# One core, attention and FFN: the last five blocks of the down weights looked up one at a time, and a higher look-up rate in gate and up

## The chip, the core and the metric

The kernel runs on one NeuronCore of a Trainium2 chip. It is one program with five instruction streams: PE (matrix multiplies into PSUM), DVE (element-wise work and all table look-ups), ACT (activations, copies out of PSUM and casts), POOL (here little more than the DMAs that it issues) and SP (most DMAs). The streams run side by side and wait for each other by semaphores; each works through its own instructions in the order in which they were written. The metric is the device time of one execution in microseconds. The time before is the median of three runs, 1115.92 us (1115.61 to 1116.86).

## The reference

The input x is 2 x 2048 x 512 in float32. A layer norm, an attention over the feature axis (the scores are 512 x 512 for each batch) and a residual come first. The feed-forward part follows, and its weights are not given as numbers but as indices into a table of 16 values:

```python
def _ghost_linear(x, idx, lut):
    w = lut[idx]
    return jnp.einsum('bsh,oh->bso', x, w)
...
gate = _ghost_linear(x, gate_idx, lut)      # gate_idx: 1376 x 512, values 0..15
up = _ghost_linear(x, up_idx, lut)          # up_idx: 1376 x 512
h = jax.nn.silu(gate) * up
return _ghost_linear(h, down_idx, lut)      # down_idx: 512 x 1376
```

The result is x + attention(norm(x)), and to that the feed-forward part of its norm is added.

## The kernel before

**Stages.** The program runs through the norm and the Gram matrices of x, a few products of 512 x 512 matrices, the attention's output y for 32 blocks of rows, then gate and up, then down. Products are made by Winograd's form of Strassen's scheme: a product of two-by-two blocks takes seven multiplies instead of eight, and sums of the operands (S1 to S4 for the left one, T1 to T4 for the right one) that DVE makes beforehand.

**Gate and up.** The 1376 inner features are cut into 11 blocks (`FT`, line 84; ten of 128 and one of 96); f counts them from 0. For each f there are four units, one for each pair p of chunks of rows (`GateUp`, line 819). A unit has seven stages: a1, c1, a2, c2, b, a3 and a4, each one product of two matrix multiplies 512 columns wide. `Line.run` (line 884) writes them in the order a1, c1, a4 of the unit before, a2, c2, b, a3. After each stage it calls `between`. Beside the products, ACT copies results out of PSUM (p1, p7, u2) and makes the two SiLUs (h0, h1); DVE makes the add for c21 and the product for h1 at stage c2, the add for h0 at stage b, and the add for c22 and the product for h0 at stage a3. The product a4 is written into the PSUM bank that c22's add reads. SP stores h to DRAM, and down reads it back.

**The look-ups.** A job (`Job`, line 191) turns up to 1024 columns of indices into weights. POOL fetches the indices by DMA (`fetch`, two buffers), ACT casts them to 16 bits (`cast`), and DVE then runs 19 instructions (`ops`): two masks in 16 bits (one step), a shift, a third mask, eight picks (a `tensor_scalar` that chooses between two neighbours of the table by the lowest bit of the index) and seven merges (a `copy_predicated` on a mask). A gate-and-up job `gu(f)` looks up a block's gate and up weights, 1024 columns (768 for the last block), and makes four sums of them. A down job `wd` looks up two blocks of 512 columns each (one for the last).

**The order of the work.** It is written out by hand. The list `jobs` (lines 300 to 302) fixes the order of the look-ups. `looked_up` (line 304) is a generator which hands out one DVE step at a time with an estimated cost in microseconds. `pump(us)` (line 321) adds us to a credit and takes steps until the credit is used up; the last step may overshoot, and the overshoot is owed:

```python
owed[0] = min(owed[0] + us, 2 * us + 1.0)
while owed[0] > 0:
    cost = next(lookup, None)
    if cost is None:
        return
    owed[0] -= cost
```

A job `gu(f)` has a gate: it may start only once block f-2 has been written out (`f < 2 + passed[0]`, line 282), since there are two buffers for a block's weights. While the gate is closed the list stands, and `pump` returns. Tenth step of a job (`k == 9`): the next job's indices are cast. End of a job: the indices of the job two further on are fetched.

`between` (line 917) runs a prepared piece of other work if there is one (20 of them, all in block 0), and else calls `pump`. At the start of block f the loop (line 1095) makes sure that the weights are there, by handing out whatever is left of the list up to them, without any stage of PE between:

```python
while "S4" not in gu[f]:
    next(lookup)
```

The down weights are first used in the sums at the start of the last block of gate and up (`down_sums`, line 951).

Of the kernel before, what the change touches and what calls it, by code (L numbers as in the profile page):

```python
# [58 lines left out]
def tile_attn_ffn(  # L59
# [24 lines left out]
    FT = [(f, min(P, INTER - f)) for f in range(0, INTER, P)]  # L84
    NFT = len(FT)
    NPAIR = NFT // 2
# [20 lines left out]
    wd = wdp.tile([P, NFT, E], F32, tag="wd", name="wd")  # L107
# [143 lines left out]
    def gu_job(f):  # L251
        f0, rows = FT[f]
        n = KB * rows

        def load(queue, idx):
            queue.dma_start(idx[:, :n], gate_idx[:, KB * f0 : KB * f0 + n])
            queue.dma_start(idx[:, n:], up_idx[:, KB * f0 : KB * f0 + n])

        def dest():
            gu[f] = {  # L260
                "w": wgu.tile([P, 2, KB, P], F32, tag="w", name=f"w_{f}"),
                "s": wgu.tile([P, 3, 2, P], F32, tag="s", name=f"s_{f}"),
            }
            flat = gu[f]["w"].rearrange("p g k r -> p (g k r)")[:, : 2 * n]
            gu[f]["flat"] = flat
            return flat

        def after():
            flat = gu[f]["flat"].rearrange("p (g k r) -> p g k r", g=2, k=KB)
            a11, a12 = flat[:, 0, 0:2, :], flat[:, 0, 2:4, :]  # L270
            a21, a22 = flat[:, 1, 0:2, :], flat[:, 1, 2:4, :]
            s1, s2, s4 = (gu[f]["s"][:, q, :, :rows] for q in range(3))
            for op, d, u, v in (
                (add, s1, a21, a22), (sub, s2, s1, a11), (sub, a21, a11, a21), (sub, s4, a12, s2)
            ):
                op(d, u, v)
                yield 0.42
            gu[f].update(
                {"11": a11, "12": a12, "S3": a21, "22": a22, "S1": s1, "S2": s2, "S4": s4}
            )  # L280

        return Job(f"gu{f}", P, 2 * n, load, dest, after, lambda: f < 2 + passed[0])

    def down_job(i):
        f0, rows = FT[2 * i]
        n = 2 if i < NPAIR else 1

        def load(queue, idx):
            queue.dma_start(
                idx.rearrange("p (o e) -> p o e", o=n),  # L290
                down_idx[f0 : f0 + n * rows, :].rearrange("(o p) e -> p o e", o=n),
            )

        def dest():
            return wd[:rows, 2 * i : 2 * i + n, :].rearrange("p o e -> p (o e)")

        return Job(f"wd{i}", rows, n * E, load, dest, lambda: iter(()), lambda: True)


    jobs = [gu_job(0), gu_job(1)] + [down_job(i) for i in range(3)]  # L300
    jobs += [gu_job(2), gu_job(3), down_job(3), gu_job(4), down_job(4), gu_job(5), gu_job(6)]
    jobs += [down_job(NPAIR)] + [gu_job(f) for f in range(7, NFT)]

    def looked_up():

# [15 lines left out]
    def pump(us):  # L321
# [7 lines that stand above are left out]
# [555 lines left out]
    class Line:  # L884


        def __init__(self, between):
            self.last, self.between = None, between
# [28 lines left out]
    def between():  # L917
        if todo:
            todo.pop(0)()
        else:  # L920
            pump(0.9)


    def late(i, loads=(), turns=(), pair=None):
# [163 lines left out]
    def by_two(ops):  # L1088
        return [
            lambda v=ops[i : i + 2]: [op() for op in v] for i in range(0, len(ops), 2)  # L1090
        ]

    line = Line(between)
    for f in range(NFT):
        while "S4" not in gu[f]:
# [102 lines left out]
```

## Time and profile before

| what | value |
|---|---|
| median of three runs | 1115.92 us (1115.61 to 1116.86) |
| the profiled execution, its own time | 1115.62 us |
| its span, first to last instruction | 1113.8 us |
| mean granted PE clock | 0.995 |
| busy: PE, DVE, ACT, POOL | 1089.8, 695.1, 303.6, 32.1 us (98%, 62%, 27%, 3%) |
| HBM traffic over the span | 105 GB/s |

The profile's page splits the span among the engines, and lists the costliest groups of instructions by the line that made them. In the groups' names, a_g, b_g and c_g are the PSUM tiles of gate and up, a_d, b_d and c_d those of down, w and s a block's weights and their sums, gu and wd the tiles of the look-ups, and idx, b the indices in 32 and 16 bits. Line 814 is the helper that issues the multiplies, lines 125 and 128 the helpers for a difference and a sum, line 230 the pick and line 242 the merge. Each multiply in float32 shows as two records, so a stage of gate and up is four. In a line of waits, the three figures are the total in us, how many times, and the longest. The time outside the span, 1115.62 - 1113.8 = 1.8 us, is the start and end of the execution.

### The profile page before, as it was taken

To read this page: it belongs to the slowest core of one execution; us is meant where nothing else is said; L and a number is where in the kernel's file an instruction comes from. 1 tells how busy PE (TensorE), PEld (TensorE's weight loads), DVE (VectorE), ACT (ScalarE), POOL (GpSimd) and SP (SyncE) were. 2 spreads that over 40 slices of the span, in tenths; PEclk is the share of its full clock that TensorE was granted. 3 is DMA by queue.
4 is the path that set the end of the run, shared out by engine and by line. 5 is a ranking of instruction groups with operands and counts; after the bars stand their busy time and mean duration, and the time that the engine had idled before them with its cause. 6 is when DMAs were issued, how large, how long until landed. Compare 5 with 4: busy or idle time off the path is not lost.

```text
span 1113.8 us, 10427 instructions
## 1 busy us (share of the span) xinstructions
PE 1089.8 (98%) x3516; PEld 654.0 (59%) x3516; DVE 695.1 (62%) x1267; ACT 303.6 (27%) x567; POOL 32.1 (3%) x63
## 2 busy tenths in 40 slices
PE   7999999999999999999699999999999999999998
PEld 4668886444444444444244444444437888888887
DVE  6967787777576587788687675755552344433341
ACT  4642522565532223223122222222221000000000
POOL 0000000000230000000000000000000000000000
PEclk9999999999999999999899999999999999999999
DMA  8461203445741111111021111111315543345511
GB/s 339 174 223 46 50 19 109 157 131 184 257 154 38 67 66 39 61 61 66 26 67 67 56 48 62 39 47 48 137 49 178 161 156 129 103 161 169 159 64 38
DMA packets 80116, 117.15 MB, mean 105 GB/s; under 512 B 16432, under 2 KB 36912, under 8 KB 78144
## 3 DMA queue, kind: packets, MB, share of 16 engines
q1 hardware_dynamic: 76848, 106.99, 28.3%
q0 software_dynamic: 3216, 9.51, 2.9%
q8 instruction: 27, 0.44, 0.2%
q14 instruction: 25, 0.20, 0.1%
HBM read 64.56 MB, written 51.90 MB: 105 GB/s over the span
## 4 chain that ended last, share of the span: by engine, by line
PE 92%; DVE 3%; DMA 3%; ACT 1%; issue 1%; SPq 0%; POOL 0%; DVEq 0%; POOLq 0%; ACTq 0%
PE a_g L814 25%; PE a_d L814 14%; PE c_g L814 13%; PE y L686 9%; PE c_d L814 7%; PE gp L372 6%; PE b_g L814 6%; PE b_d L814 4%; DMA fl<-xnd 2%; PE ea_t L521 1%; PE ea_p L521 1%; PE ea_m L521 1%; PE ea_s L521 1%; PE xt L718 1%; PE ec_t L521 1%; PE ec_m L521 1%
## 5 line engine op out<-in xcount | busy, mean ns | idle before, releaser
L128 DVE TENSOR_TENSOR c<-c_g,u 128x512 f32<-128x512 f32 (+1 forms) x44 | 30.3, 690 | 142.9 <-PE c_g L814 136.1
L686 PE MATMUL y<-m,nT 128*128 128x512 f32 x256 | 112.8, 592 | 0.0
L814 PE MATMUL a_g<-xb,w 128*128 128x512 f32 (+1 forms) x176 | 84.6, 604 | 9.6 <-DVE w L242 9.6
L814 PE MATMUL c_g<-xb,w 128*128 128x512 f32 (+1 forms) x176 | 84.1, 600 | 1.4 <-DVE w L125 0.8
L814 PE MATMUL a_g<-xb,s 128*128 128x512 f32 (+1 forms) x176 | 82.9, 593 | 1.0 <-DVE c L128 1.0
L814 PE MATMUL a_g<-xT_a,s 128*128 128x512 f32 (+1 forms) x176 | 82.8, 592 | 0.0
L814 PE MATMUL b_g<-xb,w 128*128 128x512 f32 (+1 forms) x176 | 82.7, 592 | 0.0
L372 PE MATMUL gp<-xn_a 128*128 128x512 f32 (+3 forms) x256 | 71.7, 443 | 7.1 <-ACT xn_a L183 7.1
L686 PEld LDWEIGHTS y<-m,nT 128*128 128x128 f32 x256 | 47.4, 190 | 52.7 <-issue 52.1
L866 ACT ACTIVATE h<-h 128x512 f32<-128x512 f32 (+1 forms) x44 | 27.7, 630 | 166.3 <-DVE h L128 166.3
L372 PEld LDWEIGHTS gp<-xn_a 128*128 128x128 f32 x256 | 44.9, 195 | 33.5 <-issue 16.5
L814 PEld LDWEIGHTS a_g<-xb,w 128*128 128x128 f32 (+1 forms) x176 | 33.4, 191 | 53.0 <-issue 42.3
L814 PE MATMUL a_g<-xT_sq,s 128*128 128x512 f32 (+1 forms) x132 | 62.0, 592 | 0.0
L814 PEld LDWEIGHTS c_g<-xb,w 128*128 128x128 f32 (+1 forms) x176 | 33.4, 191 | 45.8 <-issue 42.2
L230 DVE TENSOR_SCALAR gu<-idx_gu,lut_x,lut_sb 128x1024 int32<-128x1024 int32 (+1 forms) x77 | 59.2, 795 | 0.0
L814 PEld LDWEIGHTS a_g<-xb,s 128*128 128x128 f32 (+1 forms) x176 | 32.8, 188 | 44.4 <-issue 38.6
L814 PEld LDWEIGHTS b_g<-xb,w 128*128 128x128 f32 (+1 forms) x176 | 33.0, 188 | 42.5 <-issue 42.5
L814 PEld LDWEIGHTS a_g<-xT_a,s 128*128 128x128 f32 (+1 forms) x176 | 32.9, 188 | 42.7 <-issue 42.0
L242 DVE COPY_PREDICATED gu<-b_gu,gu 128x1024 f32<-128x1024 int16 (+1 forms) x44 | 56.3, 1280 | 0.8
L814 PE MATMUL a_d<-dT,hs_a 128*128 128x256 f32 x224 | 56.2, 379 | 0.0
L242 DVE COPY_PREDICATED wd<-b_wd,wd 128x1024 f32<-128x1024 int16 (+1 forms) x42 | 51.0, 1215 | 0.7
L843 ACT COPY p<-a_g 128x512 f32<-128x512 f32 (+1 forms) x44 | 25.7, 584 | 83.7 <-PE a_g L814 83.7
(240 smaller groups left out, 1726.2 us busy)
## 6 DMA issues: line engine op xcount, KB each, us to landing
hd<-h SPq DMA_DIRECT2D x80, 256.0 KB, 2.0
h<-hd SPq DMA_DIRECT2D x40, 512.0 KB, 6.5
nl<-nd SPq DMA_DIRECT2D x128, 64.0 KB, 2.1
x1d<-x SPq DMA_DIRECT2D x8, 1024.0 KB, 4.5
r<-x1d SPq DMA_DIRECT2D x32, 256.0 KB, 4.2
out_dram<-r SPq DMA_DIRECT2D x32, 256.0 KB, 2.5
x<-in_x_dram SPq DMA_DIRECT2D x7, 1024.0 KB, 13.4
nd<-xn_a SPq DMA_DIRECT2D x20, 256.0 KB, 2.1
```

The costliest lines, as they stand in the source:

```text
L128: nc.vector.tensor_tensor(dest, a, b, ALU.add)
L230: vec.tensor_scalar(dest.bitcast(I32), idx, lut_x[:rows, k : k + 1], lut_i[:rows, at : at + 1], ALU.bitwise_and, ALU.bitwise_xor,)
L242: vec.copy_predicated(dest, masks[level - 1], t)
L372: nc.tensor.matmul(gp[b][i][:, i * P :], xn[:, i * P : (i + 1) * P], xn[:, i * P :], start=c % CPB == 0 and j == 0, stop=c % CPB == CPB - ...
L521: nc.tensor.matmul(ps[:, m, :], self.a[a][:, k, m * P : (m + 1) * P], self.b[b][:, k, :], start=first and m == k == 0, stop=k == 1, skip_g ...
L686: nc.tensor.matmul(ys[k], nTs[k][:, i, :], m[:, i, :], start=(i == 0), stop=(i == KB - 1))
L718: nc.tensor.transpose(ps[:, i * P : (i + 1) * P], xfs[k][:, i * P : (i + 1) * P], ident)
L814: nc.tensor.matmul(ps, lhsT, rhs, start=first and i == 0, stop=i == len(pairs) - 1, skip_group_check=not first,)
L843: nc.scalar.copy(self.p1, self.a)
L866: nc.scalar.activation(self.h0, self.h0, AF.Silu)
```

## The change

Two things change. First, the down weights of blocks 0 to 5 are still looked up in three jobs of two blocks each, but blocks 6 to 10 are now looked up in five jobs of one block (before: blocks 6 and 7, 8 and 9 in two jobs of two, block 10 in one). `down_job` takes the first block and the number of blocks. The new order of the list after the first five jobs is gu2, gu3, wd6, gu4, wd7, gu5, wd8, gu6, wd9, gu7, wd10, gu8, gu9, gu10; before it was gu2, gu3, wd6-7, gu4, wd8-9, gu5, gu6, wd10, gu7, gu8, gu9, gu10. Second, `between` pays 1.0 instead of 0.9 for each stage.

```diff
-    def down_job(i):
-        f0, rows = FT[2 * i]
-        n = 2 if i < NPAIR else 1
+    def down_job(i, n=1):
+
+        f0, rows = FT[i]
...
-            return wd[:rows, 2 * i : 2 * i + n, :].rearrange("p o e -> p (o e)")
+            return wd[:rows, i : i + n, :].rearrange("p o e -> p (o e)")
...
-    jobs = [gu_job(0), gu_job(1)] + [down_job(i) for i in range(3)]
-    jobs += [gu_job(2), gu_job(3), down_job(3), gu_job(4), down_job(4), gu_job(5), gu_job(6)]
-    jobs += [down_job(NPAIR)] + [gu_job(f) for f in range(7, NFT)]
+    jobs = [gu_job(0), gu_job(1)] + [down_job(i, 2) for i in range(0, 6, 2)] + [gu_job(2)]
+    for i in range(6, NFT):
+        jobs += [gu_job(i - 3), down_job(i)]
+    jobs += [gu_job(f) for f in range(NFT - 3, NFT)]
...
         if todo:
             todo.pop(0)()
         else:
-            pump(0.9)
+            pump(1.0)
```

## The prediction

> **What bounds the kernel now.** I read the page's busy shares first: PE 98%, DVE 62%, ACT 27%, a mean PE clock of 0.995. So PE sets the end, and only PE's gaps can be won. Second, the waits of PE between 340 and 840 us, the stretch of gate and up:
>
> ```profile
> PE a_g L814 <- DVE w L242: 9.6, 1, 9.6
> PE c_g L814 <- DVE w L125: 0.8, 1, 0.8
> PE a_g L814 <- DVE c L128: 0.8, 1, 0.8
> ```
>
> Two of the three are waits for w, the looked-up weights of a gate-and-up block; the third, 0.8, is the last product at 837 us, which the change does not touch. Third, the chain of waits around them (start, us, what):
>
> ```profile
> 477.60 3.43 PE a_g L814 x8
> ...
> 488.30 0.35 DVE w L125
> 488.65 0.04 issue
> 488.69 1.98 PE c_g L814 x4
> 490.68 3.43 PE a_g L814 x8
> ...
> 526.73 3.43 PE a_g L814 x8
> ...
> 538.12 1.29 DVE gu L242
> ...
> 543.53 1.31 DVE w L242
> 544.84 0.04 issue
> 544.88 3.78 PE a_g L814 x4
> 548.66 2.84 PE c_g L814 x4
> 551.50 3.43 PE a_g L814 x8
> ```
>
> A stage (one product) is four records and 1.72 us; a unit is seven stages, and its marker, an eight-record a_g (a4 and a2), returns every 12.02 us (502.69, 514.71, 526.73). A block is four units, 48.07 us. Block 4 begins near 486 us, block 5 near 535: 477.60 to 490.68 is 13.08, so 1.06 is lost; 526.73 to 551.50 is 24.77, so **12.75** is lost. Together **13.8 us**. From 551.50 to the marker at 827.89 are 276.39 us, exactly 23 units; nothing else is lost. Fourth, busy times by stretch (width; PE, PEld, DVE, ACT, POOL busy; PE clock; DMA share; GB/s):
>
> ```profile
> 392.00:440.00 48.00, 48.00 (x113) 21.28 (x112) 38.26 (x54) 13.75 (x23) 1.11 (x2) 1.00 0.15 55
> 536.00:545.00 9.00, 0.12 (x1) 0.12 (x1) 8.83 (x11) 0.67 (x1) 0.53 (x1) 0.75 0.15 51
> 545.00:548.70 3.70, 3.70 (x5) 1.63 (x6) 3.67 (x10) 0.00 (x0) 0.00 (x0) 0.50 0.02 4
> ```
>
> While PE stands, DVE does nothing but look-ups, and PE then restarts at half clock: the 12.75 is 9.57 of standing plus (3.78-1.72)+(2.84-1.72) = 3.18 of slow products. In block 2 (392 to 440), with DVE at 38.26 of 48, PE lost nothing.
>
> **Why DVE is late there.** The kernel's own costs say it. A gate-and-up job is 0.74+0.65+0.37, eight picks of 0.75, seven merges of 1.27, four sums of 0.42: 18.33 us. A two-block down job is the same without sums, 16.65; a one-block job has the same 19 instructions at half width: 0.47+0.375+0.235+8x0.475+7x0.685 = 9.68. A block pays 28 stages x 0.9 = 25.2. gu(f) may begin only in block f-1, and what stands behind it in the list waits too. Block 1: gu2, then gu3 is not yet allowed, 6.9 unused. Block 2: gu3 and 6.87 of wd3. Block 3: 9.78 of wd3 and 15.42 of gu4, 2.9 missing less the last step's overshoot: two sums are forced out at block 4 (the 1.06). Block 4: wd4, 16.65, then half of gu5; 9.0 forced out at block 5 (the chain shows just these merges). Later blocks carry at most 20.4.
>
> [...] 0.50 in 545 to 548.7 after 9.57 us; the 0.8 us gap cost no clock. [...] pick 808 ns at 1024 columns, 537 at 512; merge 1312 and 731. [...] In this trace, amid look-ups, the index DMAs issue in 0.53 to 0.85 us and land in 3.1 to 4.0 (medians)[...].
>
> **The change part by part.**
>
> ```profile
> L242 DVE COPY_PREDICATED wd<-b_wd,wd 128x1024 f32<-128x1024 int16 x14 | 18.4, 1312 | 0.3
> L230 DVE TENSOR_SCALAR wd<-idx_wd,lut_x,lut_sb 128x1024 int32<-128x1024 int32 x16 | 12.4, 808 | 0.0
> ...
> L242 DVE COPY_PREDICATED wd<-b_wd,wd 96x512 f32<-96x512 int16 x7 | 5.1, 731 | 0.2
> ...
> L230 DVE TENSOR_SCALAR wd<-idx_wd,lut_x,lut_sb 96x512 int32<-96x512 int32 x8 | 4.0, 537 | 0.0
> ```
>
> *Splitting.* Blocks 6 to 9 go from two wide jobs to four narrow ones; block 10 was narrow. By durations a wide job is 2x0.421+0.69+0.42+8x0.808+7x1.312 = 17.6, a narrow one 2x0.284+0.42+0.28+8x0.537+7x0.731 = 10.7 (measured on 96 rows; I take the same for 128, bounds 10.7 and, no cheaper than its columns, 8.8). DVE gains 38 instructions and 4x10.7-2x17.6 = +7.6 us. ACT gains two casts net: four at 0.62 for two at 1.05, +0.4. POOL gains two index DMAs at 0.7: +1.4. The first five jobs and gu2 keep their places, so nothing before 344 us moves.
>
> *Order and rate.* A block now has 28.0 to spend and, in blocks 2 to 6, gu(f+1) with one narrow job: 28.01; blocks 1 and 7 to 9 hold gate and up alone. At the start of a block the credit is up to 3.0, because the gate had stopped the list. Going through list and stages, gu(f+1) ends at stage 15 of 28 and the narrow job at 25; nothing is forced out at any boundary, with 12 stages, 20 us, in hand. Both gaps go: **-13.8**. After block 9 no job is left, as before, so the rate does nothing in down.
>
> *What hides the additions.* DVE in block 1, with gu2 alone, is 30.34 us busy; a narrow job adds 10.7 by durations, and 9.8 after the overlap that block 1's total shows (33.0 by durations for 30.34). So 40.2 of 48.07: 84%, 1.9 above block 2, where PE lost nothing. Cost on the path 0; were there no cover, 7.6.
>
> *The order on DVE.* More look-ups now stand in front of the adds that free PSUM. The tightest: a4 overwrites the bank that the add of c22 reads, two stages (3.43) after a3. From the end of c2, DVE does two operations (1.2), one stage's look-ups, h0 (0.6), another stage's, then c22 (0.7). Two stages' look-ups are at most 2.0 plus an overshoot of 1.3. So c22 ends at 5.8 at the latest, and a4 begins at 3.43+3.43 = 6.87: 1.1 in hand. DVE must be free at the end of c2: its idle time there is now 1.5 to 3.0 in looked-up stretches, less 7x0.1 = 0.7. Cost 0, bound 0.2 a unit.
>
> *Fetches.* ACT's cast of the next job stands in front of ACT's copies of PSUM. The index DMA goes out after the last pick of the job two before; from there to the cast are, after a gate-and-up job, 3.81+1.68+5.03 = 10.5 us of cost, 18 us of stages, against 2x0.54+3.5 = 4.6. After a narrow job it is 2.06+8.57, as long. Cost 0.
>
> Sum: the profiled execution, 1115.62, less 13.8 is 1101.8 (span 1100.0); the median of the runs shown lies 0.3 above the profiled one: **1102.0**. What is late next is nothing on DVE: PE runs back to back from 344 us to the end.
>
> **Rivals.** *A new wait on PSUM in place of the old ones.* DVE at 84% makes c22 late by some 0.2 us in each of 20 units of blocks 2 to 6: +4, 1106. For: DVE is in order, and the margin 1.1; against: block 2 at 38.26 without a gap. *A cast waits for its indices:* ACT stands until the fetch lands. PE stops once ACT is 3.4 late; five casts, each 0.5 beyond that, give 2.5: 1104.5. Against: 18 us of lead. *Slower: DVE becomes the bound of blocks 2 to 6.* It decides once their look-ups and adds need over 48.07 us; to eat the gain and 2.2 more takes 3.2 a block, a DVE need of 51.3, so a narrow job of some 21 us, twice the measured row. It would give 1118. *The forced look-ups stay* (the list is held elsewhere than I count): 1116.
>
> **How the numbers follow.** Forecast 0.84, PSUM wait 0.06, cast 0.05, DVE bound 0.02, gaps stay 0.03. The forecast alone spans 1101 to 1103.5; the low end takes 1 us for the runs' spread (1115.61 to 1116.86), the high end the cast and most of the PSUM case: 1100.7 to 1105.0. 0.2%, 2.2 us, is about what can be told from no change. Faster 0.95, same 0.03, slower 0.02.
>
> **What would show it.** PE's waits for w gone from the stretch; markers 12.02 us apart from 344 us on; no clock under 1.00 near 540; DVE about 40 busy in blocks 2 to 6; span near 1100. Wrong if PE waits for c L128 in many units, if ACT waits at its cast for a DMA, or if a wait for w remains at a block's start.

## The result and the profile after

The changed kernel takes **1101.64 us** (median of four runs, 1100.71 to 1102.65), the kernel before 1115.76 in the same comparison: a ratio of 0.9879, 95% interval 0.9867 to 0.9891. The profiled execution took 1100.71 us with a span of 1098.9. The forecast was 1102.0, in a range of 1100.7 to 1105.0.

The waits of PE in the stretch of gate and up, all of them (total in us, times, longest):

```profile
PE a_g L815 <- DVE c L128: 0.8, 1, 0.8
PE c_g L815 <- DVE xb L125: 0.4, 1, 0.4
```

The two waits for w are gone. What is left is the last product of gate and up, which was there before, and 0.4 us in block 0. (The helper of the multiplies is now line 815, since the diff adds a line.)

The chain of waits over the place of both old gaps (start, us, what):

```profile
488.67 3.43 PE a_g L815 x8
...
500.69 3.43 PE a_g L815 x8
...
512.70 3.43 PE a_g L815 x8
...
524.72 3.43 PE a_g L815 x8
...
536.74 3.43 PE a_g L815 x8
```

The marker of a unit comes every 12.02 us, through the starts of blocks 4 and 5 too. No line of DVE is in this part of the chain.

The busy times by stretch (width; PE, PEld, DVE, ACT, POOL; PE clock; DMA share; GB/s):

```profile
344.00:392.00 48.00, 48.00 (x114) 21.21 (x113) 30.33 (x44) 12.87 (x21) 0.56 (x1) 1.00 0.14 50
392.00:440.00 48.00, 48.00 (x113) 21.23 (x112) 39.37 (x63) 13.38 (x22) 1.62 (x3) 1.00 0.17 60
...
536.00:584.00 48.00, 48.00 (x113) 21.28 (x112) 39.42 (x63) 13.39 (x22) 1.60 (x3) 1.00 0.16 59
```

PE is busy throughout at full clock. DVE works 39.4 of 48 us in every block with a down job, and 30.3 in a block without.

### The profile page after: what moved, and what is told of

The parts are those of the page before. It is cut to its first block, busy times and chain, and to the rows that moved or that the text cites. A ratio compares the mean times of both kernels' runs of the same rounds, so it can differ in the third digit from the quotient of the medians.

```text
span 1098.9 us, 10474 instructions
## 1 busy us (share of the span) xinstructions
PE 1085.8 (99%) x3516; PEld 652.9 (59%) x3516; DVE 699.5 (64%) x1305; ACT 303.9 (28%) x569; POOL 32.9 (3%) x65
## 4 chain that ended last, share of the span: by engine, by line
PE 93%; DMA 3%; DVE 2%; ACT 1%; issue 1%; SPq 0%; POOL 0%; DVEq 0%; POOLq 0%; ACTq 0%
PE a_g L815 26%; PE a_d L815 14%; PE c_g L815 13%; PE y L687 9%; PE c_d L815 7%; PE gp L373 6%; PE b_g L815 6%; PE b_d L815 4%; DMA fl<-xnd 2%; PE ea_t L522 1%; PE ea_p L522 1%; PE ea_m L522 1%; PE ea_s L522 1%; PE xt L719 1%; PE ec_t L522 1%; PE ec_p L522 1%
## 5 line engine op out<-in xcount | busy, mean ns | idle before, releaser
L128 DVE TENSOR_TENSOR c<-c_g,u 128x512 f32<-128x512 f32 (+1 forms) x44 | 30.3, 690 | 120.7 <-PE c_g L815 120.7
L242 DVE COPY_PREDICATED wd<-b_wd,wd 128x512 f32<-128x512 int16 (+2 forms) x56 | 53.1, 949 | 0.9
L128 DVE TENSOR_TENSOR r<-r,a_d 128x256 f32<-128x256 f32 x32 | 13.5, 421 | 54.8 <-PE a_d L815 54.8
## 6 DMA issues: line engine op xcount, KB each, us to landing
x<-in_x_dram SPq DMA_DIRECT2D x7, 1024.0 KB, 13.8
```

The costliest lines, as they stand in the source:

```text
L128: nc.vector.tensor_tensor(dest, a, b, ALU.add)
L242: vec.copy_predicated(dest, masks[level - 1], t)
```

## The experiments

A loss is a run's median less the changed kernel's 1101.64. The kernel before ran beside each group: 1115.65 us beside the first four runs below, 1115.36 beside the old list at 1.1 and the run with less work, 1115.23 beside the other four.

**The rate alone** (the kernel before, 1.0 for 0.9):

```diff
-            pump(0.9)
+            pump(1.0)
```

> The old list of wide jobs, 1.0 a stage. My theory (only look-ups forced out at a block's start cost time): counting the costs through the stages, block 4 has nothing left over and block 5 only the four sums of gu5. As at block 4 of the kernel before, that costs about 1.1 us, so 1102.7 us: the rate alone brings nearly the whole gain, the split about 1 us. Rival (the split carries the gain, since wide jobs stand in front of gate-and-up jobs): 1108 us or more, half of the gain or less.

Measured: 1106.02 us (1103.52 to 1106.33), ratio to before 0.9905 (0.9888 to 0.9921). The place was right, block 5 and nothing at block 4, but the loss is 4.4 us and not 1.1. DVE around the start of block 5 (start, us, engine, line, operation):

```profile
533.09 1.30 DVE L242 COPY_PREDICATED gu<-b_gu,gu 128x1024 f32<-128x1024 int16 x1
534.27 0.68 DVE L128 TENSOR_TENSOR c<-a_g,p 128x512 f32<-128x512 f32 x1
534.87 0.69 DVE L872 TENSOR_TENSOR h<-h,c 128x512 f32<-128x512 f32 x1
535.47 1.30 DVE L242 COPY_PREDICATED w<-b_gu,gu 128x1024 f32<-128x1024 int16 x1
536.80 0.42 DVE L128 TENSOR_TENSOR s<-w 128x256 f32<-128x256 f32 x1
```

PE's first product of the block, and the chain there (start, us, what):

```profile
536.82 2.90 PE L814 MATMUL a_g<-xb,w 128*128 128x512 f32 x4 [2.67 <-DVE w L242]
```

```profile
525.57 3.43 PE a_g L814 x8
...
536.82 2.90 PE a_g L814 x4
539.73 2.49 PE c_g L814 x4
542.22 3.43 PE a_g L814 x8
```

Two things were missing in my count. The last merge into w was not forced out, it had been handed out by the last stage's own pump; but that put it on DVE behind the add of c22 and the product for h0, so the first product waits for it just the same, 2.67 us. And after this wait PE ran at reduced clock (0.66 on average from 536.5 to 540.5). The markers at 525.57 and 542.22 stand 16.65 apart: 4.63 lost, 2.67 of it waiting and 1.96 slow products. The slow products do not come every time: three executions with a mean clock of 0.998 took 1105.74 to 1106.33 us, and the fourth, at 1.000, took 1103.52.

**The list alone** (the changed kernel at 0.9; the same line turned back).

> The new list of single blocks, still 0.9 a stage. My theory: the five one-block jobs cost 28.0 a block against 25.2 paid, and the debt comes out late: the four sums of gu7 at block 7 (1.1 us) and a merge and four sums of gu8 at block 8 (PE waits 0.7 + 0.6 + 1.3 = 2.6 us). Sum 3.7, so 1105.3 us, with no wait for w at blocks 4 and 5. Rival (the rate carries the gain): near 1113 us.

Measured: 1109.28 us (1107.72 to 1112.65), ratio 0.9945 (0.9925 to 0.9965), a loss of 7.6. The places were again right, and each costs more than I had counted:

```profile
PE a_g L815 <- DVE w L242: 6.1, 2, 3.4
```

The two waits for w are at the starts of blocks 7 and 8, near 631 and 683 us, and the clock in the 3.5 and 4.0 us after them is 0.51 and 0.59. The profiled execution is the slowest of the four. In the two fastest, 1107.72 and 1108.18 us, the mean clock is 1.000, and their loss is about the 6.1 us of waiting alone. The rival's 1113 lies just above the slowest run; the list alone brings about half of the gain.

**Two entries moved** (the kernel before: wide jobs, 0.9):

```diff
-    jobs += [gu_job(2), gu_job(3), down_job(3), gu_job(4), down_job(4), gu_job(5), gu_job(6)]
-    jobs += [down_job(NPAIR)] + [gu_job(f) for f in range(7, NFT)]
+    jobs += [gu_job(2), gu_job(3), down_job(3), gu_job(4), gu_job(5), down_job(4), gu_job(6)]
+    jobs += [gu_job(7), down_job(NPAIR)] + [gu_job(f) for f in range(8, NFT)]
```

> Wide jobs and 0.9 a stage as in the kernel before; only two entries of the list are moved: the job of blocks 8 and 9 behind gu5, and that of block 10 behind gu7. My theory: forced out are two sums at block 4 and four sums at block 6, 1.1 us each, so 1103.7 us without either half of the change. Rival (width or rate is needed): 1110 us or more.

Measured: 1107.07 us (1105.05 to 1107.48), ratio 0.9918 (0.9903 to 0.9933). Block 4 costs what it did before, a wait of 0.8 us; block 6 has a wait of 2.6 for w and the slow products behind it, clock 0.51 from 586 to 589.5, where the first product takes 3.60 us. So it took longer than the expected 1103.7 for the same two reasons as the rate alone: the last merge into w stands on DVE behind the block's last add and last product, and slow products follow. Still, neither the width nor the rate was needed for 8.6 us of the gain.

**The new width at the old rate, down jobs spread** (the changed kernel):

```diff
-    for i in range(6, NFT):
-        jobs += [gu_job(i - 3), down_job(i)]
-    jobs += [gu_job(f) for f in range(NFT - 3, NFT)]
+    jobs += [gu_job(3), down_job(6), gu_job(4), down_job(7), gu_job(5), gu_job(6), down_job(8)]
+    jobs += [gu_job(7), down_job(9), gu_job(8), gu_job(9), down_job(10), gu_job(10)]
...
-            pump(1.0)
+            pump(0.9)
```

> Single blocks at 0.9 a stage, but one down job is set back where the debt grows: gu3, wd6, gu4, wd7, gu5, gu6, wd8, gu7, wd9, gu8, gu9, wd10, gu10. My theory: nothing is forced out at any block, so the same time as the changed kernel, 1101.6 us, and no wait of PE for w. Rival (a higher rate has a worth of its own): 1103 us or more.

Measured: 1102.15 us (1101.96 to 1102.28), ratio 0.9877 (0.9863 to 0.9892), as expected. There is no wait for w; by the count each gate-and-up job is done by stage 24 at the latest. With the list spread like this, the higher rate has no worth of its own.

**The old list at 1.1 a stage** (wide jobs).

> The old list of wide jobs at 1.1 a stage. Counting the costs through the stages, every gate-and-up job is done by stage 21 of the block before. My theory (a block's weights must be done in time, and nothing else): the same as the changed kernel, 1101.6 us, with no wait of PE for w, so the split is not needed. Rival (wide jobs cost something by their 1.3 us merges in front of the adds): 1104 us or more.

Measured: 1101.71 us (1101.29 to 1102.73), ratio 0.9877 (0.986 to 0.9893), and no wait for w. So the split is not needed either. Neither half is indispensable; what counts is that the weights of a block are done before DVE reaches the last add of the block before it.

**The old list at 0.95 and at 0.8 a stage.**

> The kernel before with 0.95 a stage. My theory: a pick, three merges and four sums of gu5 are forced out at block 5. PE waits for c22 and h0 (1.3), the pick (0.8) and the merges (3.9), 6.0 us, and then runs at half clock for a while, another 2 to 3.2 us: 1110 us. If the half clock costs nothing after 6 us: 1107.6 us.

Measured: 1111.46 us (1110.7 to 1113.87), ratio 0.9972 (0.996 to 0.9983). PE waits 7.2 us for w at block 5, 1.2 more than summed, and the clock is 0.50 from 542 to 547.5. The 1107.6 without a cost of the slow clock is below every run.

> The kernel before with 0.8 a stage. My theory: block 4 waits for a pick and three merges (6.0 us and about 3 of slow clock), block 5 for six merges and four picks (1.3 + 7.9 + 2.9 = 12.1 and 3.2 of slow clock), block 7 for one sum (about 1): 25 us above the changed kernel, 1127 us. If idle PE time alone counts: 1121 us.

Measured: 1127.91 us (1127.33 to 1128.59), ratio 1.0115 (1.0099 to 1.0132):

```profile
PE a_g L814 <- DVE w L242: 20.1, 2, 12.9
```

The two waits, 20.1, are 2.0 over the sum of 18.1; with the slow products behind them (3.53 us for the first after the shorter wait; 3.78 and 2.48 for the first two after the longer, where others take 1.72) the loss is 26.3 us, near the expected 25. Block 7 has the third wait, 0.3. With the kernel before, 0.8, 0.9, 0.95, 1.0 and 1.1 a stage give 1127.9, 1115.8, 1111.5, 1106.0 and 1101.7: the fewer look-ups the stages pay for, the longer PE stands, until at 1.1 no wait is left.

**Less work on DVE** (the one-block jobs stop after four picks and three merges):

```diff
-            yield from pick(4, 0, w)
+            yield from pick(3 if self.cols == E else 4, 0, w)
```

> The changed kernel with the one-block down jobs cut to their first four picks and three merges: the weights of blocks 6 to 10 are looked up only in part, so this part of the computation is left out. It takes about 4 us of DVE out of each of blocks 2 to 6. My theory (PE alone sets the time there): no change from the changed kernel, 1101.6 us. Rival (some of DVE's load still costs PE something): 1100 us or less.

Measured: 1101.62 us (1100.54 to 1102.87), ratio 0.9874 (0.9859 to 0.9889). DVE falls from 39.4 to 34.9 us a block, and the time doesn't move. So the look-ups that were left out, about half of each of these jobs, had cost PE nothing.

**More work on DVE** (each one-block job makes its picks and merges twice, at 1.4 a stage):

```diff
             yield from pick(4, 0, w)
+            if self.cols == E:
+                yield from pick(4, 0, w)
...
-            pump(1.0)
+            pump(1.4)
```

> The changed kernel; each one-block down job makes its eight picks and seven merges twice (the result is the same), with 1.4 a stage so that nothing is forced out. A block of gate and up then needs about 39.4 + 8.5 = 47.9 us of DVE out of 48.07. My theory (DVE has 8 us of room a block): at most 1 us lost a block, 1102 to 1107 us. Rival (DVE is near its bound at 40, since it also waits for PE): 8.5 us more in each of five blocks less the little idle time, 1130 us or more.

Measured: 1107.68 us (1106.65 to 1108.23), ratio 0.9935 (0.992 to 0.9949). A block by its busy times, DVE's waits from 340 to 640 us, and PE's from 340 to 890:

```profile
392.00:440.00 48.00, 47.33 (x111) 20.56 (x110) 46.97 (x76) 12.60 (x21) 1.62 (x3) 1.00 0.15 55
```

```profile
DVE c L128 <- PE c_g L817: 14.4, 2, 7.3
DVE c L128 <- PE a_g L817: 4.7, 8, 1.0
DVE h L128 <- PE b_g L817: 1.1, 3, 0.4
```

```profile
PE a_g L817 <- DVE c L128: 3.5, 6, 0.8
```

DVE is at 47.0 of 48 and hardly waits for PE in blocks 2 to 6 any more, and yet PE loses only 1.2 us a block ((1107.68-1101.64)/5). The 0.8 among PE's waits is the last product of gate and up, as before; the other five, one a block, are about 0.55 us each, for c22. In the chain the marker behind such a wait comes 0.81 late, and one other marker of the block 0.40 late, behind a gap too short for the list of waits. The time is just over the expected range, and far from the rival's 1130: nearly all of the 8 us of room a block was there to use. As the rate rose with the load, to 1.4, the run doesn't say which of the two the 1.2 us come from.

**The same work, bunched** (the changed kernel at 2.0 a stage).

> The changed kernel with 2.0 a stage: the same look-ups, bunched in the first half of each block. My theory of the add that frees PSUM: with 5.0 of credit at a block's start and 2.0 a stage, DVE falls behind, c22 of the first unit ends about 2 us after a4 could begin, that of the second another 2.5: 4.5 us in each of blocks 2 to 6, 2 us in blocks 1, 7, 8 and 9, so 1125 to 1135 us, slower than the kernel before, with PE waiting for c L128. Rival (what counts is DVE's sum over a block, 40 of 48 us): 1102 us.

Measured: 1160.73 us (1156.5 to 1162.23), ratio 1.0405 (1.0382 to 1.0429), **slower than the kernel before**, by more than I expected. PE's waits, and the clock at one of them:

```profile
PE a_g L815 <- DVE c L128: 37.3, 15, 3.5
```

```profile
409.00:414.00 5.00, 1.50 (x5) 0.42 (x3) 4.96 (x7) 1.10 (x2) 1.08 (x2) 0.87 0.46 157
414.00:419.50 5.50, 5.50 (x7) 2.40 (x8) 5.40 (x13) 1.18 (x2) 0.00 (x0) 0.50 0.13 48
```

Not one wait is for w: every block's look-ups are done long before they are needed. PE waits for c22 instead, up to 3.5 us, as DVE works through look-ups that were handed out ahead of the adds; and after the wait of 3.5 us that ends at 413.96 the products run at half clock; in the stretches of 48 us from 344 to 680 the mean clock is 0.93 to 0.97. So the sum over a block doesn't decide alone; what stands in front of the add does. The profile's span, 1154.7, is 55.8 over the changed kernel's: 36.5 of it are waits (37.3 less the 0.8 of the last product, which the changed kernel has too), for which I had summed 30.5 (5x4.5 and 4x2). Another 18.7 are slow products, which I had left out: PE is busy for 1104.5 us here, at a mean clock of 0.985, and for 1085.8 in the changed kernel, at 1.000.

## Why the prediction was right

**The gaps go: right.** The prediction took 1.06 and 12.75 us from the markers; after the change the markers are 12.02 us apart at both places. Of the span's 14.9 us the two gaps explain 13.8. Most of the remaining 1.1 lies ahead of block 1: the marker in the last unit of block 0 is at 333.40 us before and at 332.45 after, 0.95 earlier. The list stands at gu2's gate there (no look-up runs from 262 to 341 us in either trace), so neither half of the change has anything to do. This marker lies anywhere from 332.4 to 334.9 us in the twelve traces, and both 332.45 and 334.40 occur with the new list: it is scatter between executions. The profiled execution so came out 1.1 us under the forecast for it, and the median 0.9 above that execution, where 0.3 was assumed; that the median hit the forecast within 0.4 us is in part luck.

**Why DVE was late: right.** The count of costs named the blocks where look-ups were left over in the kernel before, and in five further lists or rates it named the block of each wait, though not its length. That the slow clock was part of the loss holds as well: 9.57 us of standing cost 12.75.

**The split costs 7.6 us of DVE: right.** The narrow rows for 128 partitions, which the trace before didn't have, take the same as those for 96, 733 ns where those took 731 and 538 where they took 537:

```profile
L242 DVE COPY_PREDICATED wd<-b_wd,wd 128x512 f32<-128x512 int16 x28 | 20.5, 733 | 0.5
L230 DVE TENSOR_SCALAR wd<-idx_wd,lut_x,lut_sb 128x512 int32<-128x512 int32 x32 | 15.9, 538 | 0.0
```

**Hidden: right.** 39.4 us of DVE a block were measured for 40.2 forecast, and leaving out 4.5 of them changes nothing.

**The order on DVE: right, with more in hand.** In block 3 after the change, DVE has c21, then h1, a merge, h0, a merge and c22:

```profile
445.86 0.69 DVE L128 TENSOR_TENSOR c<-c_g,u 128x512 f32<-128x512 f32 x1 [1.54 <-PE c_g L815]
...
450.05 0.68 DVE L128 TENSOR_TENSOR c<-a_g,p 128x512 f32<-128x512 f32 x1
```

c22 ends 4.9 us after c2's end, where the bound was 5.8; a4 begins at 452.46, 1.7 us later, and in none of the 20 units of blocks 2 to 6 is it less. The rival, a new wait on PSUM, did not happen at 1.0, but both the doubled and the bunched look-ups show it: PE waits 2.7 us for c22 with the first and 36.5 with the second.

**The fetches: right.** No wait of ACT for an index DMA shows between 340 and 840 us; the indices of the one-block jobs land in 2.8 us (median for 128 rows).

**The slower rival** set its point at a DVE need of 48.07 us a block. The doubled jobs went to about that and lost 1.2 a block, so the point was well placed for a load spread like that. The bunched run shows that the same end can be reached at 40 us, by order alone; of that the prediction's rival said nothing.

**What I had wrong in the expectations of the runs**, and would have had wrong in the prediction of a smaller change: I took only what is forced out at the start of a block as late. What the last stage hands out stands on DVE behind the block's last add and last product, and is late too; and already the wait of 2.67 us was followed by 1.96 us of slow products.

## What to carry to other kernels

Where one engine prepares operands for the next block in slices between stages, add up for each block what the stages pay and what its jobs cost, in the order of the list, and keep the next block's job first and done some stages early; a job that is not due (here the wide down job in front of gate and up) should not stand ahead of one that is. Spread that work evenly: too little a stage leaves a gap at the block's start, too much a stage puts it ahead of the operations that free PSUM, and the second can cost more than the first (here 1160.73 us at 2.0 a stage, 1127.91 at 0.8). When the bound engine is PE, price a gap with the slow products that can follow it (here 3.18 us behind 9.57 of standing, 1.96 behind 2.67).

## What the runs showed of the hardware

After a wait of 2.67 us, 1.96 us of slow products followed (the rate alone; clock 0.66 from 536.5 to 540.5). Beside waits of 0.8 us and less no slow clock shows: it is 1.00 from 488 to 491, around the restart after the wait of 0.80 in the kernel before, and 1.000 on average with the doubled jobs, which have a wait of about 0.55 in each of five blocks. Each still cost about 0.26 more than its length: 1.06 us for the wait of 0.80, 0.81 for that of 0.55.

In between, the length alone doesn't decide. In the bunched run PE works 1.50 us from 409 to 414 and is at half clock after that, as shown there; it works 1.51 us from 465 to 470 and keeps its full clock:

```profile
465.00:470.00 5.00, 1.51 (x4) 0.47 (x3) 4.97 (x7) 1.69 (x3) 1.07 (x2) 1.00 0.45 154
470.00:475.00 5.00, 5.00 (x13) 2.13 (x13) 4.90 (x12) 2.13 (x3) 0.00 (x0) 1.00 0.14 52
```

Executions of one kernel differ in this too, as the mean clocks of the rate alone show (three of 0.998, one of 1.000). What decides was not shown.

The longer waits in the stretch of gate and up were each followed by slow products: those of 7.2 us (the old list at 0.95 and at 0.8), 9.57 (the kernel before) and 12.9 (at 0.8). In the kernel before the half clock sets in while PE still stands, and lasts 5.9 us beyond its restart at 544.88:

```profile
536.00:540.40 4.40, 0.00 (x0) 0.00 (x0) 4.37 (x7) 0.67 (x1) 0.00 (x0) 1.00 0.16 60
540.60:550.80 10.20, 5.92 (x7) 2.52 (x8) 9.99 (x15) 0.58 (x1) 0.53 (x1) 0.50 0.07 21
550.80:552.00 1.20, 1.20 (x4) 0.57 (x3) 0.01 (x1) 0.41 (x1) 0.00 (x0) 1.00 0.00 0
```
